# Seven products for eight in the first keys and queries of a linear attention, and output products moved out of crowded rounds

## The chip, the cores and the metric

The kernel runs on one core of a Trainium2 chip. The metric is the device time of one execution in microseconds (us). Engines are named as in the profile: PE is the matrix engine TensorE, PEld its weight loads, DVE is VectorE, ACT is ScalarE, POOL is GpSimd, SP is the engine that issues most transfers. All data are 32-bit floats; the profile counts two matmul instructions for each product that the program asks for.

## The reference

Four layers work one after the other on x of shape (4, 512, 64, 64): four images, 512 channels, 4096 pixels. Cut to what matters:

```python
# layer 0: softmax attention with 64 channels, all pixels against all pixels
t = einsum('oc,bchw->bohw', w_qkv, x)
key_, query, value = ...                       # 64 channels each
attn = softmax(einsum('bdk,bdq->bkq', key_, query), axis=1)
x = scale * (w_out @ (value @ attn)) + x
# layer 1: 1x1, 3x3, 1x1 convolutions (512 -> 128 -> 128 -> 512), whose weights are
# mixed from 8 experts by a router on the mean of x; batch norm, relu, residual
x = relu(bn(conv3(relu(bn(conv2(relu(bn(conv1(x)))))))) + x)
# layer 2: linear attention with 64 channels
Q = softplus(Wq @ x + bq);  K = softplus(Wk @ x + bk);  V = Wv @ x + bv
x = x + gamma * (Q @ (K @ V)) / (Q @ (K.sum(-1) + EPS))
# layer 3: a projection to 2 x 512 channels, two discounted running sums, a gate
x = x + gamma3 * x_gate * sigmoid(cumsum_w(cumsum_h(x_scan)))
```

## The kernel before

The kernel holds one image in SBUF at a time, as four tiles `xs[0..3]` of 128 partitions x 4 channel groups x 1024 pixels (a "pair" of blocks of 512 pixels). Three double banks of PSUM (`pair_psum`) and two single ones (`bank`) go round among all products. PE's order is the program's; that of DVE and ACT is the program's in the stretches named `manual_schedule` and a scheduler's elsewhere. The start:

```python
    for queue, k in ((nc.scalar, 0), (nc.sync, 2)):
        queue.dma_start(wqkv_sb[:, k:k + 2, :], wqkv_t[:, k:k + 2, :])
    prm_sb = const.tile([P, NPRM], F32, tag="prm", name="prm_sb")
    nc.scalar.dma_start(prm_sb, prm)           # 50 columns of parameters
    ...
    xs = [load_pair(0, pr) for pr in range(NPAIR)]
    ...
    nc.scalar.activation(bn_s, bn_v, AF.Sqrt)  # batch norm from the parameters
    nc.vector.reciprocal(bn_v, bn_s)
```

Layer 0's first pair of keys and queries is already made with Strassen's products (in Winograd's form). Its steps for the first image, where a digit is a product, "v" a value product, "t" a sum of x, "seed" the copy of product 1 to where product 2 is added:

```python
first = ("zero v0:0 1:0 v0:1 1:1 seed v0:2 2:0 v0:3 2:1 t5 5 c11 v1:0 v1:1 t6 v1:2 v1:3 cp01 t7 6 e2 "
         "v2:0 v2:1 t4 7 e3 c22 tr01 n5 4 c21 n6 3 c12 n7 v2:2 v2:3 n4")
```

The attention of layer 0 runs in 16 rounds of eight score tiles each; what a round does after its scores:

```python
for g in range(NPAIR * NT // ROUND):
    for i in range(g * ROUND, (g + 1) * ROUND):
        scores(i)                              # two matmuls, Exp on ACT, sum on DVE
    if 1 < g < 2 + 2 * KC:
        pool(...)                              # one mean on ACT
    ended = None
    while done < (g + 1) * ROUND - (RING - ROUND):
        pr = values(done)                      # two matmuls
        done += 1
        if pr is not None:                     # the last key tile of a pair of query blocks
            ended = pr
            if pr < NPAIR - 2:
                late += [(g + 1, lambda pr=pr, m=m: out_step(pr, m)) for m in range(KC)]
    ...
    if ended is not None:
        sums(ended)                            # den on PE; reciprocal, product, two reductions on DVE
    if late and late[0][0] <= g:
        late.pop(0)[1]()                       # out_step: y on PE, x += y on DVE
```

The end of layer 1 and the head of layer 2:

```python
def conv3(pr, h2):
    for m in range(KC):
        y = pair_psum(f"c3_{b}_{pr}_{m}")
        for h in range(2):
            nc.tensor.matmul(y[:, h, :], wc[:, KC + 9 + m, :], h2[:, h, :], start=True, stop=True)
        xm = xs[pr][:, m, :]
        nc.vector.scalar_tensor_tensor(xm, flat(y), bn_s[:, 2 + m:3 + m], xm, ALU.mult, ALU.add)
        nc.scalar.activation(xm, xm, AF.Relu, bias=bn_t[:, 2 + m:3 + m])

def feature_part(w, pair, z, i, k0, n):        # w: 0 queries, 1 keys
    for kc in range(k0, k0 + n):
        for h in range(2):
            nc.tensor.matmul(z[h * D:(h + 1) * D, i, :], wqk_sb[:, kc, w * D:(w + 1) * D],
                             xs[pair[i]][:, kc, h * NB:(h + 1) * NB], start=kc == 0, stop=kc == KC - 1)

def softplus(w, pair, z, in_parts=False):
    ...
    nc.scalar.activation(e, z, AF.Abs, bias=col(BQ2 + w))
    nc.scalar.activation(pos, z, AF.Relu, bias=col(BQ2 + w))
    nc.scalar.activation(e, e, AF.Exp, scale=-1.0)
    nc.vector.tensor_scalar(u, e, 1.0, None, ALU.add)
    # then Ln on ACT; softplus_end: four DVE operations more

    h2[2] = conv2(2)
    conv3(1, h2[1])
    h2[3] = conv2(3)
    weights = load_quarters(b)
    features(1, (0, 1))()()                    # first keys, with their softplus
    conv3(2, h2[2])
    ...
    rest = features(0, (0, 1))                 # first queries
    with tc.manual_schedule(engines={mybir.EngineType.DVE}):
        key_transpose((0, 1))                  # ktr on PE, kt by DVE
        rest = rest()
        move(0, 0)                             # xtr: transposes of x on PE, then a copy xt
        move_by_halves(0, 1)
        conv3(3, h2[3])
        g = bank(f"g_{b}", (P, C))
        keys = features(1, (2, 3))             # last keys
        rest()
        keys = keys()
        products(0, ahead(1))                  # moves (0,2) and (0,3), then g += kt x xt
        keys()
        ...
```

Of the kernel before, what the change touches and what calls it, by code (L numbers as in the profile page):

```python
# [15 lines left out]
P = 128  # L16
# [30 lines left out]
def unshifted(ctx: ExitStack, tc: tile.TileContext, fits, x, wqkv_t, wout_t, router_t,  # L47
# [19 lines left out]
    def four(name):  # L67
        return fourp.tile([P, 2, NB], F32, tag="four", name=name)

    def block(name, shape=(P, NB)):  # L70
        return blkp.tile(list(shape), F32, tag="blk", name=name)
# [14 lines left out]
    def load_pair(b, pr):  # L86
        if b and pr == NPAIR - 1:
            places[NPAIR - 1:] = places[NPAIR], places[NPAIR - 1]
        t = places[pr]
        src = x[b, :, pr * 2 * NB:(pr + 1) * 2 * NB].rearrange("(kc p) n -> p kc n", p=P)  # L90
        if b == 0:
            for kc in range(KC):
                nc.sync.dma_start(t[:, kc, :], src[:, kc, :])
        else:
            nc.sync.dma_start(t, src)
        return t
# [4 lines left out]
    for queue, k in ((nc.scalar, 0), (nc.sync, 2)):  # L101
        queue.dma_start(wqkv_sb[:, k:k + 2, :], wqkv_t[:, k:k + 2, :])
    prm_sb = const.tile([P, NPRM], F32, tag="prm", name="prm_sb")
    nc.scalar.dma_start(prm_sb, prm)
    def col(i, n=1):
        return prm_sb[:, i:i + n]

    xs = [load_pair(0, pr) for pr in range(NPAIR)]

    a11, a12, a21, a22 = (wqkv_sb[:, k:k + 2, w * D:(w + 1) * D] for w in range(2) for k in (0, 2))  # L110
    wout_sb = const.tile([P, C], F32, tag="wout", name="wout_sb")
# [237 lines left out]
    def layer0(b, xs, pro):  # L349
# [106 lines left out]
        with tc.manual_schedule(engines={mybir.EngineType.Activation}):  # L456
            for g in range(NPAIR * NT // ROUND):
                for i in range(g * ROUND, (g + 1) * ROUND):
                    scores(i)
                if 1 < g < 2 + 2 * KC:  # L460
                    pool(NPAIR - 2 + (g - 2) // KC, (g - 2) % KC)
                if g == 1:
                    pro.key_copies()
                ended = None
                while done < (g + 1) * ROUND - (RING - ROUND):
                    if done == NPAIR * NT - 5:
                        inverse_sums(NPAIR - 1)
                    pr = values(done)
                    done += 1
                    if pr is not None:  # L470
# [3 lines that stand above are left out]
                if b == 0 and g == 1:  # L474
                    router = router_of_values()
                if b == 0 and g == 2:
                    router()
                if ended is not None:
                    sums(ended)
                if late and late[0][0] <= g:  # L480
                    late.pop(0)[1]()
        assert not late

# [60 lines left out]
    def layer1(b, xs, wcq, sel, rw, ex4, ex7):  # L544
# [98 lines left out]
                                     AF.Relu, bias=bn_t[:, 1:2], scale=bn_s[:, 1:2])  # L643
            return h2

        def conv3(pr, h2):
            for m in range(KC):
                y = pair_psum(f"c3_{b}_{pr}_{m}")
                for h in range(2):
                    nc.tensor.matmul(y[:, h, :], wc[:, KC + 9 + m, :], h2[:, h, :], start=True, stop=True)  # L650
# [3 lines that stand above are left out]
# [9 lines left out]
    def layer2(b, xs, sums_of_six, mix_last, conv2, conv3, wcq, qs):  # L663
# [14 lines left out]
        def features(w, pair):  # L678
            z = pair_psum(f"z_{b}_{w}_{pair[0]}")
            for i in range(2):  # L680
                feature_part(w, pair, z, i, 0, KC)
            return lambda: softplus(w, pair, z)

        def softplus(w, pair, z, in_parts=False):
            i = 2 * (len(kts) // 2 % 2)
            e, u = sp[:, i], sp[:, i + 1]
            pos, ln = four(f"pos_{b}_{w}_{pair[0]}"), four(f"ln_{b}_{w}_{pair[0]}")
            nc.scalar.activation(e, z, AF.Abs, bias=col(BQ2 + w))
            nc.scalar.activation(pos, z, AF.Relu, bias=col(BQ2 + w))
            nc.scalar.activation(e, e, AF.Exp, scale=-1.0)  # L690
            nc.vector.tensor_scalar(u, e, 1.0, None, ALU.add)
            def logarithm():
                nc.scalar.activation(ln, u, AF.Ln)
                return lambda: softplus_end(w, pair, e, u, pos, ln)
            return logarithm if in_parts else logarithm()
# [37 lines left out]
        def move(pr, j):  # L733
            xtr = pair_psum(f"xtr_{b}_{pr}_{j}")
            for h in range(2):
                n0 = h * NB + j * P
                for kc in range(KC):
                    nc.tensor.transpose(xtr[:, h, kc * P:(kc + 1) * P], xs[pr][:, kc, n0:n0 + P], ident)  # L738
            xt = four(f"xt_{b}_{pr}_{j}")
            (nc.scalar.copy if j % 2 or (pr > 1 and j) else nc.vector.tensor_copy)(xt, xtr)  # L740
            moved.append(xt)

        def products(pr, between=()):
            for j0 in range(0, TPB, 2):
                for step in [lambda j=j: move(pr, j) for j in (2, 3)] if j0 == 0 else between:
                    step()
                for j in range(j0, j0 + 2):
                    t = pr * TPB + j  # L750
                    xt = moved.pop(0)
                    for h in range(2):
                        nc.tensor.matmul(g[h * D:(h + 1) * D, :], kts[pr][:, j, h * D:(h + 1) * D], xt[:, h, :],  # L753
                                         start=t == 0, stop=t == NPAIR * TPB - 1)

        def ahead(pr):
            return [lambda j=j: move(pr, j) for j in range(2)]

        with tc.manual_schedule(engines={mybir.EngineType.DVE}):
            sums_of_six(0)  # L760
            sums_of_six(1)
            sums_of_six(2)
            mix_last()
            h2 = {0: conv2(0)}
            sums_of_six(3)
            h2[1] = conv2(1)
            conv3(0, h2[0])
        h2[2] = conv2(2)
        conv3(1, h2[1])
        h2[3] = conv2(3)  # L770
        weights = load_quarters(b)
        features(1, (0, 1))()()
        conv3(2, h2[2])


        def invert(pair):
# [14 lines left out]
            q = qs[:, pair[0]:pair[1] + 1, :]  # L791
            nc.vector.tensor_tensor(q, q, nrm, ALU.mult)

        rest = features(0, (0, 1))
        with tc.manual_schedule(engines={mybir.EngineType.DVE}):
            key_transpose((0, 1))
            rest = rest()
            move(0, 0)
            move_by_halves(0, 1)
            conv3(3, h2[3])  # L800
            g = bank(f"g_{b}", (P, C))
            keys = features(1, (2, 3))
            rest()
            keys = keys()
            products(0, ahead(1))
            keys()
            products(1, ahead(2))
            kfold = bank(f"kfold_{b}", (P, NPAIR))
            nc.tensor.matmul(kfold, fold, ks, start=True, stop=True)
            ksum = small.tile([P, 1], F32, tag="ksum", name=f"ksum_{b}")  # L810
            nc.vector.tensor_reduce(ksum, kfold, AX.X, ALU.add)
            for h in range(2):
                r = slice(h * D, (h + 1) * D)
                nc.vector.tensor_scalar(kbd[r, 16 * h:16 * (h + 1)], ones[r, 0:16], ksum[r, :], 1e-6, ALU.mult, ALU.add)
            key_transpose((2, 3))
            inv = invert((0, 1))
            products(2, ahead(3))
            divide((0, 1), inv)
            weights[2]()
            products(3)  # L820
            g_sb = block(f"gsb_{b}", (P, C))
            nc.scalar.copy(g_sb, g)
            gt = block(f"gt_{b}", (P, KC, P))

            late = (0, (2, 3), pair_psum(f"z_{b}_0_2"))
            feature_part(*late, 0, 0, 2)

            gk = pair_psum(f"gk_{b}")
            for kc in range(KC):
                nc.tensor.matmul(gk[:, 0, kc * P:(kc + 1) * P], g_sb[:, kc * P:(kc + 1) * P], fold,  # L830
                                 start=True, stop=True)
            nc.scalar.copy(gt, gk[:, 0, :].rearrange("p (kc c) -> p kc c", c=P))
            feature_part(*late, 0, 2, 2)
            kv = small.tile([P, C], F32, tag="kv", name=f"kv_{b}", bufs=1)
            for i in range(2):
                part = slice(i * C // 2, (i + 1) * C // 2)
                kvp = bank(f"kvp_{b}_{i}", (P, C // 2))
                for kc in range(KC):
                    nc.tensor.matmul(kvp, gt[:, kc, :], wv_sb[:, kc, part], start=kc == 0, stop=kc == KC - 1)
                nc.vector.scalar_tensor_tensor(kv[:, part], bv_sb[:, part], ksum, kvp, ALU.mult, ALU.add)  # L840
# [744 lines left out]
```

## Time and profile before

| | before |
|---|---|
| median of 3 runs | 2655.01 us (2654.95 to 2657.95) |
| span of the profiled execution | 2653.7 us |
| granted clock of PE | 0.999 |
| DVE, ACT busy | 76%, 50% of the span |

The page gives each engine's busy time and, apart from it, the chain of work that ended last. An engine's busy share says little of where time can be had; the chain and the waits of the engine that carries it say more. A line of the timeline reads: start, duration, engine, line of the kernel, operation, tile written <- tiles read, shapes, count, and in brackets the idle time before it and what ended it. Costly groups of the page that the change touches:

```profile
L376 PE MATMUL s<-qv,key 64*128 64x512 f32 x2048 | 458.0, 594 | 5.3 <-DVE x L440 3.2
```

Here the columns are the count, the busy time in us, the mean of one in ns, and the idle time of the engine just before these instructions with what ended most of it: 5.3 us in all before the scores.

### The profile page before, as it was taken

Reading aid. Unit: us, or ns where it says so; the run is one execution under the profiler, and the core shown is the slowest. Engines: PE = TensorE matmul, PEld = TensorE weight load, DVE = VectorE, ACT = ScalarE, POOL = GpSimd, SP = SyncE. Lnnn points to the kernel's source line nnn. Section 1 sums busy time; section 2 is a strip of 40 time slices with the busy share of each in tenths; the row PEclk is TensorE's granted clock in tenths of the full one; section 3 lists DMA queues with packets and bytes.
Section 4 is the critical chain, followed back from the end, with each engine's and each line's share of the span. In section 5 each row is a group of like instructions: output and inputs, shape, how many; then the busy total and the mean of one; then the engine's idle time right before and its main releaser. Section 6 shows DMA issues by size and latency. Waiting matters only on the chain.

```text
span 2653.7 us, 25809 instructions
## 1 busy us (share of the span) xinstructions
PE 2636.2 (99%) x10050; PEld 1116.5 (42%) x10050; DVE 2017.9 (76%) x2272; ACT 1316.2 (50%) x1510; POOL 12.1 (0%) x26
## 2 busy tenths in 40 slices
PE   9999999999999999999999999999999999999998
PEld 3333464344333345444433334544443333554443
DVE  7777866888777786688877778668887777856887
ACT  4554353454555436345556553535555555263545
POOL 1000000000000000000000000000000000000000
PEclk9999999999999999999999999999999999999999
DMA  5000210022200021012220002101121000210001
GB/s 193 1 1 1 103 32 1 27 101 80 80 1 1 1 103 32 1 47 80 80 80 1 1 1 103 32 1 63 64 87 72 0 1 8 97 32 1 32 40 57
DMA packets 34739, 115.17 MB, mean 43 GB/s; under 512 B 3120, under 2 KB 12080, under 8 KB 33072
## 3 DMA queue, kind: packets, MB, share of 16 engines
q1 hardware_dynamic: 34320, 113.21, 11.3%
q8 instruction: 81, 1.33, 0.2%
q14 instruction: 50, 0.41, 0.1%
q10 hardware_dynamic: 288, 0.22, 0.0%
HBM read 79.86 MB, written 33.55 MB: 43 GB/s over the span
## 4 chain that ended last, share of the span: by engine, by line
PE 96%; DVE 2%; ACT 1%; issue 0%; DMA 0%; SPq 0%; ACTq 0%
PE av L391 17%; PE sx L934 16%; PE s L376 16%; PE zy L934 12%; PE z L675 4%; PE c L650 4%; PE c L578 4%; PE c L627 3%; PE wv L852 2%; PE y L435 2%; PE kq L312 2%; PE vv L265 2%; PE g L753 2%; PE xtr L738 2%; PE c2e L627 2%; PE kqz L312 1%
## 5 line engine op out<-in xcount | busy, mean ns | idle before, releaser
L376 PE MATMUL s<-qv,key 64*128 64x512 f32 x2048 | 458.0, 594 | 5.3 <-DVE x L440 3.2
L379 ACT ACTIVATE ring<-s 128x1024 f32<-128x1024 f32 x336 | 317.2, 1050 | 260.3 <-PE s L376 260.3
L384 DVE TENSOR_TENSOR acc<-acc,ring 128x1024 f32<-128x1024 f32 x312 | 382.2, 1225 | 63.2 <-ACT ring L379 35.6
L376 PEld LDWEIGHTS s<-qv,key 64*128 64x128 f32 x2048 | 192.1, 186 | 264.0 <-issue 118.1
L391 PE MATMUL av<-ring,qv 128*64 128x512 f32 x1344 | 302.2, 595 | 0.0
L934 PE MATMUL sx<-t,x 128*128 128x512 f32 x512 | 232.4, 593 | 0.0
L384 DVE TENSOR_TENSOR acc<-acc,x 128x1024 f32<-128x1024 f32 x168 | 205.6, 1224 | 34.7 <-ACT x L379 19.4
L379 ACT ACTIVATE x<-s 128x1024 f32<-128x1024 f32 x176 | 166.7, 1053 | 124.4 <-PE s L376 124.4
L391 PEld LDWEIGHTS av<-ring,qv 128*64 128x64 f32 x1344 | 92.6, 137 | 200.1 <-issue 200.1
L939 ACT COPY zy<-sx 128x512 f32<-128x512 f32 x64 | 36.5, 570 | 253.9 <-PE sx L934 253.9
L391 PE MATMUL av<-x,qv 128*64 128x512 f32 x704 | 159.5, 595 | 0.0
L984 DVE TENSOR_TENSOR_SCAN t<-x,t 128x512 f32<-128x512 f32 x128 | 149.2, 1209 | 1.6
L934 PEld LDWEIGHTS sx<-t,x 128*128 128x128 f32 x512 | 96.7, 190 | 124.6 <-issue 120.9
L943 ACT ACTIVATE e<-sx,prm_sb 128x512 f32<-128x512 f32 x128 | 87.8, 686 | 122.4 <-PE sx L934 122.4
L967 DVE TENSOR_TENSOR_SCAN s<-wc,s 128x512 f32<-128x512 f32 x128 | 146.1, 1202 | 0.0
L973 ACT COPY t<-s 128x1024 f32<-128x1024 f32 x64 | 127.5, 1992 | 29.3 <-DVE s L967 28.7
L990 ACT ACTIVATE s<-t 128x1024 f32<-128x1024 f32 x64 | 125.7, 1990 | 11.2 <-DVE t L984 11.1
L934 PE MATMUL zy<-t,wq 128*128 128x512 f32 x256 | 118.5, 602 | 0.0
L934 PE MATMUL zy<-x,wq 128*128 128x512 f32 x256 | 118.0, 600 | 0.0
L934 PE MATMUL sx<-x,wq 128*128 128x512 f32 x256 | 117.1, 595 | 0.0
L934 PE MATMUL sx<-t,wq 128*128 128x512 f32 x256 | 116.6, 595 | 0.0
L934 PE MATMUL zy<-x,x 128*128 128x512 f32 x256 | 116.3, 594 | 0.0
(227 smaller groups left out, 3451.9 us busy)
## 6 DMA issues: line engine op xcount, KB each, us to landing
out_dram<-s SPq DMA_DIRECT2D x62, 512.0 KB, 2.6
x<-in_x_dram SPq DMA_DIRECT2D x12, 2048.0 KB, 8.4
x<-in_x_dram SPq DMA_DIRECT2D x16, 512.0 KB, 9.7
ex<-in_packed_dram SPq DMA_DIRECT2D x4, 2048.0 KB, 7.7
ex<-in_experts_dram SPq DMA_DIRECT2D x4, 2048.0 KB, 7.9
wq<-in_wproj_t_dram SPq DMA_DIRECT2D x32, 256.0 KB, 5.0
ex<-in_packed_dram SPq DMA_DIRECT2D x4, 1536.0 KB, 6.0
ex<-in_experts_dram SPq DMA_DIRECT2D x4, 1536.0 KB, 6.4
```

The costliest lines, as they stand in the source:

```text
L376: nc.tensor.matmul(s[:, h, :], key[r, kt * P:(kt + 1) * P], qry[r, pr * NB:(pr + 1) * NB], start=True, stop=True)
L379: nc.scalar.activation(p, s, AF.Exp)
L384: nc.vector.tensor_tensor(accs[pr], accs[pr], p, ALU.add)
L391: nc.tensor.matmul(avs[pr][h * D:(h + 1) * D, :], vt[:, kt, :], ring[i % RING][:, h, :], start=kt == 0, stop=kt == NT - 1)
L578: nc.tensor.matmul(y[:, h, :], wc[:, kc, :], xs[pr][:, kc, h * NB:(h + 1) * NB], start=kc == 0, stop=kc == KC - 1)
L627: nc.tensor.matmul(y[:, lo - a:hi - a], u, v[:, lo:hi], start=dy == 1, stop=dy == 2)
L650: nc.tensor.matmul(y[:, h, :], wc[:, KC + 9 + m, :], h2[:, h, :], start=True, stop=True)
L934: nc.tensor.matmul(y, w[:, c, self.kind, self.j * P:(self.j + 1) * P], v[:, c, :], start=c == 0 and k in (1, 5), stop=c == 1, skip_group_c ...
L967: nc.vector.tensor_tensor_scan(self.half(i, h), along[:, self.j + 2 * i, :], self.half(i, h), 0.0, ALU.mult, ALU.add)
L973: nc.scalar.copy(self.t[i].rearrange("p (w r) -> p w r", w=W), self.s[i].rearrange("p (r w) -> p w r", w=W))
L984: nc.vector.tensor_tensor_scan(th, down[:, i, :], th, 0.0, ALU.mult, ALU.add)
L990: nc.scalar.activation(self.s[i].rearrange("p (r w) -> p w r", w=W), tw, AF.Sigmoid)
```

## The change

It has three parts.

1. The first pair's keys and queries of layer 2 are a product of a 2 x 2 matrix of weight blocks (queries and keys by two halves of the channels) and a 2 x 2 matrix of x blocks. They are now made with seven products instead of eight. The sums of blocks are made on DVE. The four steps of the third `conv3` stand between these products, the last `conv3` right behind them, and the softplus of both runs beneath the last `conv3` and the last keys' products. The softplus of the queries takes its buffers from the tile of the sums.
2. In layer 0 an output product no longer stands in a round that has the sums of a finished pair (`elif`), which is to even out the rounds.
3. The load of the parameters is issued by SP behind the first pair of x, not by ACT at the start.

The diff, cut to its core:

```diff
-    nc.scalar.dma_start(prm_sb, prm)
-    xs = [load_pair(0, pr) for pr in range(NPAIR)]
+    xs = [load_pair(0, 0)]
+    nc.sync.dma_start(prm_sb, prm)
+    xs += [load_pair(0, pr) for pr in range(1, NPAIR)]
@@ layer 0, the rounds
                 if ended is not None:
                     sums(ended)
-                if late and late[0][0] <= g:
+                elif late and late[0][0] <= g:
                     late.pop(0)[1]()
@@ layer 2
+        def first_features(between):
+            xa, xb = ((x[:, 0:2, :], x[:, 2:4, :]) for x in xs[0:2])
+            t5, t6 = (xsum[:, i:i + 2].rearrange("p c h n -> p c (h n)") for i in (0, 2))
+            w = block(f"zw_{b}", (P, 4, 2, D))
+            ...
+            nc.vector.tensor_tensor(w5, a21, a22, ALU.add)         # and w6, w7, w3
+            ws = {1: a11, 2: a12, 3: w3, 4: a22, 5: w5, 6: w6, 7: w7}
+            ts = {1: xa[0], 2: xa[1], 3: xb[1], 4: t5, 5: t5, 6: t6, 7: t6}
+            zy, y = pair_psum(f"zz_{b}"), bank(f"zs_{b}")
+            def product(k):
+                to = y if k in (1, 6, 7, 4) else zy[:, 0 if k == 2 else 1, :]
+                for c in range(2):
+                    for h in range(2):
+                        nc.tensor.matmul(to[h * D:(h + 1) * D, :], ws[k][:, c, :], ts[k][:, c, h * NB:(h + 1) * NB],
+                                         start=c == 0 and k in (1, 5), stop=c == 1, skip_group_check=k not in (1, 5))
+            ...
+            sub(t5, xb[0], xa[0])             # two DVE operations of 1024 columns each
+            sub(t6, xb[1], t5)
+            yield
+            product(5)
+            product(1)
+            nc.scalar.copy(zy[:, 0, :], y)
+            sub(t5, xa[1], t6)
+            between(0)
+            product(2)
+            product(6)
+            e2 = copy_out(2)
+            between(1)
+            sub(t6, xb[1], xb[0])
+            between(2)
+            product(7)
+            e3 = copy_out(3)
+            between(3)
+            zq = xsum[:, 2]
+            nc.vector.tensor_tensor(zq[:, 1, :], zy[:, 1, :], e3, ALU.add)
+            product(4)
+            nc.vector.tensor_copy(zq[:, 0, :], y)
+            product(3)
+            nc.vector.tensor_tensor(zy[:, 1, :], zy[:, 1, :], e2, ALU.add)
+            yield zy, zq
         h2[2] = conv2(2)
         conv3(1, h2[1])
+        xsum = bigp.tile([P, 4, 2, NB], F32, tag="big", name=f"xsum_{b}")
+        first = first_features(lambda m: conv3(2, h2[2], (m,)))
+        next(first)
         h2[3] = conv2(3)
         weights = load_quarters(b)
-        features(1, (0, 1))()()
-        conv3(2, h2[2])
+        zk, zq = next(first)
+        rest = softplus(0, (0, 1), zq, places=(xsum[:, 0], xsum[:, 1], zq, xsum[:, 3]))
+        keys = softplus(1, (0, 1), zk)
@@
-        rest = features(0, (0, 1))
         with tc.manual_schedule(engines={mybir.EngineType.DVE}):
-            key_transpose((0, 1))
-            rest = rest()
+            conv3(3, h2[3])
             move(0, 0)
             move_by_halves(0, 1)
-            conv3(3, h2[3])
             g = bank(f"g_{b}", (P, C))
-            keys = features(1, (2, 3))
+            last_keys = features(1, (2, 3))
+            keys()
             rest()
-            keys = keys()
-            products(0, ahead(1))
+            key_transpose((0, 1))
+            move(0, 2)
+            keys = last_keys()
+            products(0, ahead(1), (3,))
             keys()
```

More of the change, by code (lines that the diff above doesn't have):

```diff
@@ L644, in conv2, with conv3 @@
             return h2
-        def conv3(pr, h2):
-            for m in range(KC):
+        def conv3(pr, h2, ms=range(KC)):
+            for m in ms:
                 y = pair_psum(f"c3_{b}_{pr}_{m}")
@@ L682, in features, with softplus @@
             return lambda: softplus(w, pair, z)
-        def softplus(w, pair, z, in_parts=False):
+        def softplus(w, pair, z, in_parts=False, places=None):
             i = 2 * (len(kts) // 2 % 2)
-            e, u = sp[:, i], sp[:, i + 1]
-            pos, ln = four(f"pos_{b}_{w}_{pair[0]}"), four(f"ln_{b}_{w}_{pair[0]}")
+            if places:
+                e, u, pos, ln = places
+            else:
+                e, u = sp[:, i], sp[:, i + 1]
+                pos, ln = four(f"pos_{b}_{w}_{pair[0]}"), four(f"ln_{b}_{w}_{pair[0]}")
             nc.scalar.activation(e, z, AF.Abs, bias=col(BQ2 + w))
@@ L741, in move, with products @@
             moved.append(xt)
-        def products(pr, between=()):
+        def products(pr, between=(), more=(2, 3)):
             for j0 in range(0, TPB, 2):
-                for step in [lambda j=j: move(pr, j) for j in (2, 3)] if j0 == 0 else between:
+                for step in [lambda j=j: move(pr, j) for j in more] if j0 == 0 else between:
                     step()
@@ L767, in layer2, with sub, copy_out @@
             conv3(0, h2[0])
+        def first_features(between):
+            xa, xb = ((x[:, 0:2, :], x[:, 2:4, :]) for x in xs[0:2])
+            t5, t6 = (xsum[:, i:i + 2].rearrange("p c h n -> p c (h n)") for i in (0, 2))
+            w = block(f"zw_{b}", (P, 4, 2, D))
+            a21, a22, a11, a12 = (wqk_sb[:, k:k + 2, i * D:(i + 1) * D] for i in range(2) for k in (0, 2))
+            w3, w5, w6, w7 = (w[:, i] for i in range(4))
+            nc.vector.tensor_tensor(w5, a21, a22, ALU.add)
+            nc.vector.tensor_tensor(w6, w5, a11, ALU.subtract)
+            nc.vector.tensor_tensor(w7, a11, a21, ALU.subtract)
+            nc.vector.tensor_tensor(w3, a12, w6, ALU.subtract)
+            ws = {1: a11, 2: a12, 3: w3, 4: a22, 5: w5, 6: w6, 7: w7}
[7 more added lines that the diff above has]
+                                         start=c == 0 and k in (1, 5), stop=c == 1, skip_group_check=k not in (1, 5))
+            def sub(to, u, v):
+                for c in range(2):
+                    nc.vector.tensor_tensor(to[:, c, :], u[:, c, :], v[:, c, :], ALU.subtract)
+            def copy_out(k):
+                e = block(f"z{k}_{b}")
+                nc.scalar.copy(e, y)
+                return e
+            sub(t5, xb[0], xa[0])
[22 more added lines that the diff above has]
+            yield zy, zq
```

## The prediction

> **What bounds the kernel now.** I read the page's busy shares first, then the chain that ended last, then the waits of PE, then its timeline in the stages that the change touches. From the page, the busy times and the chain's shares:
>
> ```profile
> PE 2636.2 (99%) x10050; PEld 1116.5 (42%) x10050; DVE 2017.9 (76%) x2272; ACT 1316.2 (50%) x1510; POOL 12.1 (0%) x26
> ...
> PE 96%; DVE 2%; ACT 1%; issue 0%; DMA 0%; SPq 0%; ACTq 0%
> ```
>
> PE is the bound nearly everywhere: 96% of the chain is matmul after matmul. So the time is the sum of PE's issue steps plus its few waits, and work on DVE or ACT counts only where PE ends up waiting for it. All waits of PE, in total, times, longest:
>
> ```profile
> PE s L376 <- DVE x L440: 3.2, 8, 0.4
> PE s L376 <- ACT ring L379: 2.1, 8, 0.3
> PE kqz L305 <- POOL ident masks.py:199: 1.5, 1, 1.5
> PE xtr L738 <- DVE xt L740: 1.0, 4, 0.2
> PE vv L265 <- DMA x<-in_x_dram: 0.8, 1, 0.8
> ```
>
> Two attention rounds of each image stall (8 = 2 x 4). One of them, PE's timeline and then DVE's:
>
> ```profile
> 175.71 1.13 PE L435 MATMUL y<-o,wout_sb 64*128 64x512 f32 x4
> 176.68 1.88 PE L376 MATMUL s<-qv,key 64*128 64x512 f32 x8
> 178.82 1.13 PE L376 MATMUL s<-qv,key 64*128 64x512 f32 x4 [0.27 <-ACT ring L379]
> 180.35 4.13 PE L376 MATMUL s<-qv,key 64*128 64x512 f32 x18 [0.40 <-DVE x L440]
> ```
>
> ```profile
> 175.83 3.36 DVE L410 RECIPROCAL rec<-den 128x512 f32<-128x512 f32 x1 [2.71 <-PE den L407]
> 179.10 1.18 DVE L440 SCALAR_TENSOR_TENSOR x<-y,prm_sb,x 128x1024 f32<-128x1024 f32 x1
> ```
>
> The output product y is ready at 176.84, but the DVE instruction that empties its PSUM pair stands behind a reciprocal of 3.36 us until 179.10. With one of three pairs held, the scores run short. PE's timeline at the head of layer 2:
>
> ```profile
> 369.32 1.43 PE L627 MATMUL c2e<-wl,wc 128*128 128x256 f32 x6
> 370.68 7.09 PE L675 MATMUL z<-x,wqk_sb 128*64 128x512 f32 x32
> 377.70 7.13 PE L650 MATMUL c<-h,wc 128*128 128x512 f32 x16
> 384.76 7.09 PE L675 MATMUL z<-x,wqk_sb 128*64 128x512 f32 x32
> 391.78 1.09 PE L714 MATMUL ktr<-ident,k 128*128 128x128 f32 x8
> ...
> 401.42 7.09 PE L675 MATMUL z<-x,wqk_sb 128*64 128x512 f32 x32
> 408.44 1.96 PE L738 MATMUL xtr<-ident,x 128*128 128x128 f32 x16
> 410.33 1.94 PE L753 MATMUL g<-xt,kt 128*64 128x512 f32 x8
> 412.20 1.09 PE L738 MATMUL xtr<-ident,x 128*128 128x128 f32 x8
> 413.53 1.09 PE L738 MATMUL xtr<-ident,x 128*128 128x128 f32 x8 [0.24 <-DVE xt L740]
> ```
>
> No wait stands between 370.68 and 412.20: this stage is pure PE work.
>
> **What the Trainium skill says.** (1) "Trainium Kernel Development and Optimization", Performance Expectations: matmul busy time is a poor measure because matmuls are pipelined. The trace agrees: a matmul here lasts 594 ns, but 32 z matmuls take 7.02 us. I therefore use start-to-start times. (2) "TensorEngine Tiling (Array Packing)", Key Properties: a change of tiling mode drains TensorE. The trace shows its price. Inside a block two 64-column matmuls pass in 0.429 us and one of 128 columns in 0.429 us. The z block takes 7.02 us instead of 32 x 0.2145 = 6.86, the conv block after it 7.06 instead of 16 x 0.429 = 6.86. So an excursion to 64 columns and back costs about 0.35 us. (3) "TensorE: Matmul & The Clock Gate", Architectural detail: ScalarE's and VectorE's queues are strict FIFO, as DVE at 179.10 shows. (4) "DMA: Bandwidth & Descriptors", Queues, rings and completion order: SP and ACT each own a row of rings on the same engines, consumed in ring order. Here x's transfers land mostly 1.28 us apart, at 5.73, 7.51, 8.80, 10.08 and 11.36 us; the longer second step is where the parameters (landed at 5.91) share the engines.
>
> **Part 1, the rounds (elif).** An output product no longer falls into a round that has the sums. The stalling rounds are those with both: the sums of pairs 1 and 2 come with a waiting product, the sums of pair 0 don't, and that round shows no wait. In start-to-start time the two stalled steps measure 0.86 and 0.99 us instead of 0.42: 0.43 + 0.57 = 1.0 us a round (more than the idle time shown, because the pipeline also refills). Two rounds x 4 images x 1.0 = 8.0 us. The moved products go to rounds 9, 13 and 14 (and neighbours), which then look like rounds 5 to 7, where product and pooling stand without a wait. So I count the whole **-8.0 us**.
>
> **Part 2, Strassen.** Before, keys and queries of the first pair are 2 blocks of 32 matmuls; after, 7 products x 8 = 56. Saved: 8 x 0.2145 = 1.72 us an image. The products are cut by single convolution steps into 4 blocks (5 and 1; 2 and 6; 7; 4 and 3). With the last keys that makes 5 excursions instead of 3: +2 x 0.35 = 0.70. Net on PE: -1.0 us an image. Laid out from 370.68 with the same steps, the first products of g end, and xtr of block 1 starts, at 411.2 instead of 412.2.
>
> DVE and ACT get more work, which must fit beneath. DVE: 8 differences of 1024 columns (1.22 each, 9.8), 4 weight sums (some 0.2 in a row, 0.8), 3 PSUM operations of 512 columns (0.69, 2.1): 12.7 us an image. In this stage (356 to 412) DVE is busy 31.4 of 56 us, so there is room in sum; the question is each deadline. Placed by hand in the order in which the built program has them, with the durations of before:
> - Term 5 and 6 are ready at 369, products at 370.7.
> - The seed copy on ACT stands behind the last h2 ReLU (ends 375), done 375.6; product 2 wants it at 376.2. Slack 0.6.
> - Term 7 waits until product 6 has read term 6, done 381.7; product 7 at 383.4.
> - The copy e3 on ACT ends 386.6; product 4 at 387.2.
> - The product's PSUM pair is held from before the last conv2 until the softplus of the keys has read it (395.3). So conv3 has two pairs: the third step of the last conv3 wants its pair at 394.3, DVE frees it at 394.1. Tight, but no wait.
> - The key transpose is at 406.6 and the keys are ready at 404. Its PSUM pair is also that of the second x transpose after it (the allocation of images 0 and 1 says so). PE wants that one 0.87 us after the key transpose ends... and the copy kt takes 1.22 plus about 0.3 of hand-over. That is a **new wait, about 0.7 us** an image, refill included.
> - In return the wait of before at 413.53 goes (0.24 idle, 0.40 in steps): its pair is now emptied about 2 us before PE wants it.
>
> Sum: -1.0 + 0.7 - 0.4 = -0.7 an image, **-2.8 us** for four.
>
> **Part 3, the parameters' load.** It goes behind the first pair's four transfers. The same bytes still precede the second pair's first transfer, so that lands at 11.4 as before, and with it the start of term 5. But the parameters now land near 10 us. ACT's square root waits for them and the seed copy stands behind it: 9.55 becomes about 10.6, while product 2 wants its result at 10.18. DVE's ten small ops on the parameters, which ran 6.54 to 7.48 before, now stand between the two halves of term 5: 0.9 us later. The two delays overlap. Start: **+0.9 us**, once.
>
> **Sum:** 2655.0 - 8.0 - 2.8 + 0.9 = **2645.1 us**.
>
> **Rivals.**
> (a) The head of layer 2 becomes bound by DVE and ACT: two PSUM pairs and in-order queues with slacks of 0.2 to 0.6 us. If one deadline slips by a microsecond, everything behind it on DVE slips too. For it: small slacks, 12.7 us more of DVE in a stage of 56 us. Against: none of my deadlines is missed but one. It would cost 1 to 2 us an image: 2649 to 2653.
> (b) The stalls of the rounds move rather than vanish, because DVE's backlog after the sums (reciprocal 3.36, product and two reductions some 1.9) meets the product one round later. Against: round 5 follows the sums of pair 0 in just this way and has no wait. It would give back up to 8 us: 2653.
> (c) The key transpose's wait doesn't appear, since the copy comes in time, and the start isn't delayed, since the parameters land sooner: 2641 to 2642.
>
> **Range and chances.** Part 1 is measured in the trace and sure to about 1 us. Part 2 may lie between -5 and +3, part 3 between 0 and +1.3. 8 in 10: 2641 to 2650. 2% would be 53 us; nothing here is near that: faster 0.01, same 0.985, slower 0.005.
>
> **What would show it.** Right: no wait of the scores for the output product's DVE step or for the ring; PE's 32-matmul z blocks gone from the head of layer 2 save one, 56 matmuls of 64 columns in four blocks; PE's wait for the copy kt, 4 times, near 0.5 us idle; the seed's product and term 5 waiting at 10 to 15 us; the first scores starting 0.9 us later than 46.5. Wrong: waits of PE for the seed or the copies e2 and e3, or for conv3's DVE step, in all four images (rival a), or scores waiting in rounds 9 and 13 (rival b).

## The result, and the profile after

The changed kernel takes 2647.66 us (median of 6 runs, 2646.06 to 2647.90), against 2654.82 (6 runs, 2653.98 to 2657.95) of the kernel before: a ratio of 0.9971, 95% interval 0.9958 to 0.9984. That is 7.2 us less, where 9.9 less was predicted (2645.1, between 2641 and 2650). Against a threshold of 2% the time is the same; as a gain the 7.2 us are clear of the noise.

The page of the changed kernel, busy times and the chain's shares:

```profile
PE 2629.0 (99%) x10018; PEld 1113.4 (42%) x10018; DVE 2066.5 (78%) x2332; ACT 1320.3 (50%) x1522; POOL 12.2 (0%) x26
...
PE 96%; DVE 2%; ACT 1%; DMA 0%; issue 0%; SPq 0%; DVEq 0%; ACTq 0%
```

PE still carries 96% of the chain. It is busy 7.2 us less; DVE has 48.6 us more to do (12.1 an image), and of that only DVE's part in two new waits of PE reaches the time. All waits of PE in the changed kernel, in total, times, longest:

```profile
PE den L408 <- DVE acc L385: 2.5, 4, 0.9
PE xtr L742 <- DVE kt L720: 1.8, 4, 0.4
PE kqz L306 <- POOL ident masks.py:199: 1.5, 1, 1.5
PE kqz L313 <- ACT kqz L318: 1.1, 1, 1.1
PE vv L266 <- DMA x<-in_x_dram: 0.4, 1, 0.4
```

The sixteen waits of the scores are gone. Two of the new lines were expected: the wait for the key transposes' copy kt, and the one for the seed copy. The first was not: den, the sums of the last pair of query blocks, now waits for DVE once in each image. PE's timeline at the head of layer 2 of the first image:

```profile
368.29 1.43 PE L628 MATMUL c2e<-wl,wc 128*128 128x256 f32 x6
369.65 1.94 PE L791 MATMUL zz<-xsum,zw 128*64 128x512 f32 x8
371.42 1.89 PE L791 MATMUL zs<-x,wqk_sb 128*64 128x512 f32 x8
373.24 1.98 PE L651 MATMUL c<-h,wc 128*128 128x512 f32 x4
375.15 1.94 PE L791 MATMUL zz<-x,wqk_sb 128*64 128x512 f32 x8
...
398.54 7.09 PE L676 MATMUL z<-x,wqk_sb 128*64 128x512 f32 x32
405.56 1.09 PE L718 MATMUL ktr<-ident,k 128*128 128x128 f32 x8
406.49 1.04 PE L742 MATMUL xtr<-ident,x 128*128 128x128 f32 x8
407.97 1.09 PE L742 MATMUL xtr<-ident,x 128*128 128x128 f32 x8 [0.44 <-DVE kt L720]
408.99 1.94 PE L757 MATMUL g<-xt,kt 128*64 128x512 f32 x8
410.86 1.97 PE L742 MATMUL xtr<-ident,x 128*128 128x128 f32 x16
```

The products stand without a wait up to 407.97. The price of a change of tiling can be seen in their steps: between the products 5 and 1 (zz to zs at 371.42), where the tile changes but not the tiling, two matmuls still pass in 0.43 us; where products and conv3 meet, the steps beside the change are 0.47 to 0.53 us, some 0.35 us in all for one excursion. The stage from the first product to the first xtr of block 1 takes 41.21 us (369.65 to 410.86); before, it took 41.52 (370.68 to 412.20), and the wait of 0.24 us right behind it is gone too.

Since PE is the chain, the distances between first matmuls on PE show where the time went. From the timelines, in us:

| | first scores | layer 0's attention (first scores to conv1), image 0; 1; 2 | conv1 to layer 2's first value product (wv), image 0 | last matmul to the end of the span |
|---|---|---|---|---|
| before | 46.47 | 252.05; 250.48; 250.48 | 150.04 | 8.89 |
| changed | 47.00 | 250.50; 249.27; 248.91 | 149.27 | 8.07 |

From layer 2's value product to the next image's scores both take 258.75 (before, the first image took 258.94). Image 3 repeats image 2 (250.48 before, 248.91 changed). So the stages that the change touches have moved, and no other stage between them. The end of the span varies from run to run: the kernel with all three repairs (below) has 8.69 us there in one execution and 7.71 in another.

### The profile page after: what moved, and what is told of

Its sections match the earlier page's. It is cut to its first block, busy times and chain, and to the rows that moved or that the text cites. A ratio compares the mean times of both kernels' runs of the same rounds, so it can differ in the third digit from the quotient of the medians.

```text
span 2644.3 us, 25822 instructions
## 1 busy us (share of the span) xinstructions
PE 2629.0 (99%) x10018; PEld 1113.4 (42%) x10018; DVE 2066.5 (78%) x2332; ACT 1320.3 (50%) x1522; POOL 12.2 (0%) x26
## 4 chain that ended last, share of the span: by engine, by line
PE 96%; DVE 2%; ACT 1%; DMA 0%; issue 0%; SPq 0%; DVEq 0%; ACTq 0%
PE sx L997 16%; PE av L392 16%; PE s L377 16%; PE zy L997 12%; PE c L651 4%; PE c L579 4%; PE c L628 3%; PE wv L915 3%; PE y L436 2%; PE g L757 2%; PE z L676 2%; PE kq L313 2%; PE vv L266 2%; PE xtr L742 2%; PE kqz L313 2%; PE c2e L628 2%
```

## The experiments

**Each part alone.** The three parts of the change, each put into the kernel before by itself, and a measurement of the tiling's price, on one chip (the kernel before: 2654.99 us, 48 runs).

The rounds alone:

```diff
-                if late and late[0][0] <= g:
+                elif late and late[0][0] <= g:
```

> The kernel before with the elif alone. Theory: the two stalled rounds of each image go (-8.0 us in start-to-start time), but the last output product now stands two rounds later, the router's small operations on its mean fall into the last round's sums, and PE waits for them before den, 4 times, about 0.8 us each with refill (+3.2): 2654.8 - 4.8 = 2650.0, with that wait of den in the trace. Rival: the wait of den in the changed kernel comes from the Strassen part, and the rounds alone give the whole -8.0: 2646.8, without a wait of den.

Measured: 2649.27 us, ratio 0.9976 (0.9968 to 0.9985): 5.7 us less, where 4.8 was expected. PE's waits:

```profile
PE den L407 <- DVE acc L384: 2.1, 4, 0.5
PE kqz L305 <- POOL ident masks.py:199: 1.5, 1, 1.5
PE xtr L738 <- DVE xt L740: 0.9, 4, 0.2
PE vv L265 <- DMA x<-in_x_dram: 0.5, 1, 0.5
```

The wait of den comes with the rounds and not with Strassen's products, so the rival falls. DVE's timeline at the end of layer 0 of the first image, kernel before:

```profile
261.25 5.21 DVE L384 TENSOR_TENSOR acc<-acc,ring 128x1024 f32<-128x1024 f32 x4
270.02 5.21 DVE L384 TENSOR_TENSOR acc<-acc,ring 128x1024 f32<-128x1024 f32 x4 [3.55 <-ACT ring L379]
275.33 5.21 DVE L384 TENSOR_TENSOR acc<-acc,x 128x1024 f32<-128x1024 f32 x4
```

and with the rounds evened out:

```profile
265.98 1.28 DVE L440 SCALAR_TENSOR_TENSOR x<-y,prm_sb,x 128x1024 f32<-128x1024 f32 x1 [2.20 <-PE y L435]
267.19 0.08 DVE L440 DVE_READ_ACCUMULATOR x<-y,prm_sb,x 128x1 f32 x1
267.31 0.17 DVE L486 TENSOR_REDUCE pooled<-pool 128x4 f32<-128x16 f32 x1
...
268.77 0.23 DVE L493 SCALAR_TENSOR_TENSOR base<-wr_sb,osum,base 128x8 f32<-128x8 f32 x1
268.92 5.21 DVE L384 TENSOR_TENSOR acc<-acc,ring 128x1024 f32<-128x1024 f32 x4
274.23 5.21 DVE L384 TENSOR_TENSOR acc<-acc,x 128x1024 f32<-128x1024 f32 x4
```

Before, DVE waits 3.55 us for the last round's exponentials and sums them as they come. Now the last output product (round 14) is added at 265.98, and with its mean the router's seven small operations become ready and run at once, down to 268.92. The eight sums start late, stay late since they follow each other without a gap, and den waits for the eighth. It is the router's operations that make them late, and not the product's own addition: ACT's first exponential of the round is ready near 267.9 (four in 3.77 us from 266.84, 1.05 us each), by when the addition is over (267.27). ACT's and PE's timeline:

```profile
266.84 3.77 ACT L379 ACTIVATE ring<-s 128x1024 f32<-128x1024 f32 x4 [7.56 <-PE s L376]
...
279.50 1.08 PE L407 MATMUL den<-acc,ones 128*64 128x512 f32 x4 [0.54 <-DVE acc L384]
```

By PE's steps in image 1, the scores got 2.31 us shorter and the wait of den cost 0.71.

Strassen's products and the new order of layer 2 alone (the changed kernel without the `elif`, and with the parameters' load at the start):

> The kernel before with the Strassen products and the new order of layer 2 alone. Theory: -0.76 us an image (1.72 saved, 0.70 for two more excursions to 64 columns, +0.6 for the wait for kt, -0.4 for the wait that goes): 2654.8 - 3.0 = 2651.8; the stalls of the scores stay (8 and 8), the wait for kt is there 4 times, no wait of den. Rival: the part alone hurts elsewhere (a later stage, or the wait of den comes with it): 2654 to 2655, with that wait shown.

Measured: 2651.80 us, ratio 0.9987 (0.9981 to 0.9994): 3.2 us less, where 3.0 was expected. PE's longest waits:

```profile
PE s L376 <- DVE x L440: 3.2, 8, 0.4
PE s L376 <- ACT ring L379: 2.1, 8, 0.3
PE xtr L741 <- DVE kt L719: 1.8, 4, 0.4
```

The stalls of the scores stay, the wait for kt is there and den doesn't wait, so the rival falls. The stretch from conv1 to layer 2's value product takes 149.28 instead of 150.04 us: 0.76 an image.

The parameters' load alone:

```diff
-    nc.scalar.dma_start(prm_sb, prm)
-    xs = [load_pair(0, pr) for pr in range(NPAIR)]
+    xs = [load_pair(0, 0)]
+    nc.sync.dma_start(prm_sb, prm)
+    xs += [load_pair(0, pr) for pr in range(1, NPAIR)]
```

> The kernel before with the parameters' load behind the first pair of x alone. Theory: the seed copy waits behind the square root, PE waits 1.1 us for it, and the first scores start at 47.0 instead of 46.5 us: +0.5, 2655.3. Rival: the earlier first transfer (x lands 0.4 us sooner) makes up for it and the time is the same within 0.2 us, or a later wait absorbs it.

Measured: 2656.03 us, ratio 1.0002 (0.9993 to 1.0010), which doesn't settle the sign. The trace shows the mechanism. DVE, ACT and PE in its timeline:

```profile
9.79 0.29 DVE L156 TENSOR_SCALAR bn_v<-prm_sb 128x1 f32<-128x1 f32 x3 [3.08 <-DMA prm_sb<-in_prm_dram]
10.12 0.21 ACT L157 ACTIVATE bn_s<-bn_v 128x6 f32<-128x6 f32 x1 [7.65 <-DVE bn_v L156]
10.23 0.58 ACT L318 COPY kqz<-kq 128x512 f32<-128x512 f32 x1
...
10.86 1.08 PE L313 MATMUL kqz<-x,wqkv_sb 128*64 128x512 f32 x4 [0.71 <-ACT kqz L318]
```

The parameters land near 9.8 us, the square root runs at 10.12, the seed copy right behind it, and PE has waited 0.71 us. The first scores stand at 46.89; what the start loses is taken up in the last section, as the start varies by itself.

The last keys' products cut into three blocks, nothing else:

```diff
-            conv3(3, h2[3])
-            keys = features(1, (2, 3))
+            z = pair_psum(f"z_{b}_1_2")
+            conv3(3, h2[3], (0,))
+            feature_part(1, (2, 3), z, 0, 0, 2)
+            conv3(3, h2[3], (1,))
+            feature_part(1, (2, 3), z, 0, 2, 2)
+            conv3(3, h2[3], (2, 3))
+            feature_part(1, (2, 3), z, 1, 0, KC)
+            keys = lambda: softplus(1, (2, 3), z)
```

> The kernel before, with the last keys' products cut into three blocks of 8, 8 and 16 matmuls between the last conv3's steps: the same matmuls, two more excursions to 64 columns an image. Theory: a change of tiling costs PE about 0.35 us an excursion, +0.70 an image, +2.8: 2657.6, without a new wait of PE. Rival: the price hides beneath other waits or weight loads when the blocks are small: within 0.5 us of 2654.8.

Measured: 2658.37 us, ratio 1.0013 (1.0005 to 1.0021): 3.4 us more, with the kernel before's list of waits unchanged. PE's timeline:

```profile
394.64 1.88 PE L650 MATMUL c<-h,wc 128*128 128x512 f32 x4
396.45 1.94 PE L675 MATMUL z<-x,wqk_sb 128*64 128x512 f32 x8
398.32 1.98 PE L650 MATMUL c<-h,wc 128*128 128x512 f32 x4
400.24 1.94 PE L675 MATMUL z<-x,wqk_sb 128*64 128x512 f32 x8
```

Eight z matmuls from 396.45 to 398.32 take 1.87 us, of which 8 x 0.2145 = 1.72 are work. The stretch from conv1 to layer 2's value product takes 150.80 instead of 150.04 us: 0.38 for each excursion, with no wait in sight. Here a change of tiling is issue time on PE that no list of waits shows.

By their medians the three parts alone add up to -5.7 - 3.2 + 1.0 = -7.9 us; the whole change took 7.2 us on the first chip and 8.3 on another. So they don't hinder each other by more than the noise.

**Repairs of the changed kernel.** Each takes away one of its three waits (on another chip than the parts; the kernel before: 2655.16 us). The expectations start from 2647.7 us; on this chip the changed kernel took 2646.95 us later (below), so that is what the repairs are compared with.

```diff
                 elif late and late[0][0] <= g:
-                    late.pop(0)[1]()
+                    for _ in range(2 if g == 10 else 1):
+                        late.pop(0)[1]()
```

> The changed kernel, but round 10 of the attention takes two output products, so that the last of them stands in round 13 and not 14. Theory: the router's operations on the mean then run a round earlier, DVE is done with the last sums in time, and the wait of den (4 times, 0.8 us each in steps) goes: 2647.7 - 3.2 = 2644.5; two products in one round cost no wait of the scores, as neither stands behind a reciprocal. Rival: DVE's backlog comes from the sums themselves, the wait stays, or two products in a round starve the scores as before: 2647 to 2652.

Measured: 2644.52 us, ratio 0.9960 (0.9947 to 0.9974): 2.4 us below the changed kernel, where 3.2 was expected. The number 2644.5 was hit because its starting point was too high. The wait of den is gone, and DVE has its gap before the last sums again:

```profile
254.94 0.17 DVE L488 TENSOR_REDUCE pooled<-pool 128x4 f32<-128x16 f32 x1
...
261.86 5.21 DVE L385 TENSOR_TENSOR acc<-acc,ring 128x1024 f32<-128x1024 f32 x4
269.56 5.21 DVE L385 TENSOR_TENSOR acc<-acc,ring 128x1024 f32<-128x1024 f32 x4 [2.49 <-ACT ring L380]
```

The router's operations run at 254.94, a round earlier. Layer 0's attention takes 248.47 us in image 2 instead of 248.91: 0.44 less, not 0.7, because behind the two products one step of the scores takes 0.62 us instead of 0.43 and the next one 0.53; over the four images the attention is 2.1 us shorter. So the cause of den's wait is where the last product stands, with the router's operations behind it, and not DVE's load from the sums.

```diff
-            ktr = pair_psum(f"ktr_{b}_{pair[0]}")
+            ktr = [bank(f"ktr_{b}_{pr}") for pr in pair]   # for the first pair of pairs; two copies kt
@@
             key_transpose((0, 1))
+            g = bank(f"g_{b}", (P, C))                     # taken after them, not before
```

> The changed kernel, but the first key transposes go to the two single banks, copied out half by half, so that the x transpose after them doesn't need their pair. Theory: PE's wait for kt (4 times 0.6 us in steps) goes: 2647.7 - 2.4 = 2645.3. Rival: g needs one of the single banks and waits for the same copy, so the wait only moves to g: 2647.7.

Measured: 2643.51 us, ratio 0.9956 (0.9942 to 0.9970): 3.4 us below the changed kernel. PE's timeline:

```profile
405.29 1.09 PE L719 MATMUL ktr<-ident,k 128*128 128x128 f32 x8
406.22 1.91 PE L747 MATMUL xtr<-ident,x 128*128 128x128 f32 x16
408.06 1.94 PE L762 MATMUL g<-xt,kt 128*64 128x512 f32 x8
```

All transposes run on and g doesn't wait either. From conv1 to layer 2's value product: 148.61 instead of 149.28 us. The rival is out. By this stretch the repair is worth 4 x 0.67 = 2.7 us. In this trace the first image's later layers take 0.73 us longer (259.48 instead of 258.75); in the later kernels with the same repair they don't.

The third repair puts the parameters' load back on ACT at the start, as in the kernel before.

> The changed kernel with the parameters' load back on ACT at the start. Theory: the wait for the seed copy goes and the first scores start 0.5 us earlier: 2647.2. Rival: no difference.

Measured: 2645.59 us, ratio 0.9966 (0.9952 to 0.9979). The wait for the seed is gone and the first scores stand at 46.42. The time is 1.4 us below the changed kernel on the same chip, whose first scores stand at 47.14. So the start is worth 0.7 us in these traces; another 0.3 lies in image 1's attention, where den waits 0.5 instead of 0.9 us, and the rest stays open.

> The changed kernel with all three: two output products in round 10, the first key transposes in single banks, the parameters' load at the start. Theory: the sums add up, -3.2 - 2.4 - 0.5: 2641.6. Rival: a wait behind them takes over and half of it is lost: 2644.5.

Measured: 2641.43 us, ratio 0.9948 (0.9934 to 0.9962): 5.5 us below the changed kernel. That the number was hit is partly luck: by the stages the parts are 2.1, 2.7 and 0.7 us, not 3.2, 2.4 and 0.5, and the starting point was 0.7 us too high. No wait of PE is left behind the start:

```profile
PE kqz L305 <- POOL ident masks.py:199: 1.5, 1, 1.5
PE vv L265 <- DMA x<-in_x_dram: 0.6, 1, 0.6
```

**Side by side.** The changed kernel, the three repairs together, and these with the two products of round 10 set apart, on the chip of the repairs (the kernel before: 2655.23 us):

> The changed kernel itself, on the same chip as the next two, for a comparison that no change of chip blurs: 2647, with the waits for den, kt and the seed as in its first trace.

> The kernel with all three repairs once more, beside the changed one: by PE's time between the same points, 4 x (0.45 + 0.67) = 4.5 us less than the changed kernel, and about 0.5 at the start: 2642. Rival: chip and day made half of the earlier distance, 2644.

> All three repairs, but of the two output products of round 10 one stands behind the scores and the other behind the values. Theory: the two steps of the scores that are 0.19 us long after two products in a row (once an image) go: -0.8, 2641. Rival: behind the scores no PSUM pair is free, as ACT is still at the exponentials, and PE waits there instead: the same or up to 1 us more.

```diff
                     scores(i)
+                if g == 10:
+                    late.pop(0)[1]()
```

Measured: 2646.95 us (ratio 0.9969, 0.9956 to 0.9981), 2641.69 (0.9949, 0.9935 to 0.9963) and 2639.20 (0.9944, 0.9930 to 0.9958). The repairs are worth 5.3 us. Setting the products apart takes 0.30 us an image from layer 0's attention (248.56 to 248.26 in image 1), where 0.2 was expected, so 1.2 of the 2.5 us are explained by it. The rest is not shown: the two kernels' runs overlap (2641.13 to 2642.79 against 2638.46 to 2642.54), and their traces differ otherwise only at the start and the end, which vary by themselves. PE's timeline of round 10 in the last kernel:

```profile
190.46 7.08 PE L376 MATMUL s<-qv,key 64*128 64x512 f32 x32
197.37 1.02 PE L435 MATMUL y<-o,wout_sb 64*128 64x512 f32 x4
198.33 1.94 PE L391 MATMUL av<-x,qv 128*64 128x512 f32 x8
```

The product stands right behind the scores without a wait, so the rival of a missing PSUM pair falls. This kernel beats both: 16.0 us below the kernel before, 7.8 below the changed one.

## Why the prediction was right, and where not

- **Part 1, the rounds, -8.0.** The mechanism was right: the product behind the reciprocal held a PSUM pair, and without it the scores run on. Their gain was even undersized: 2.31 us an image instead of 2.0, as the step behind each stalled one takes 0.53 us instead of 0.43, too, which the prediction left out. The step that failed is "which then look like rounds 5 to 7 ... So I count the whole -8.0 us". Round 14 doesn't look like them, as the last product of layer 0 releases the router's operations in front of the last sums. That gave 0.71 us back (1.06 in image 1 of the changed kernel, in both of its traces; why it is more there stays open). Together the rounds alone bring 1.54 to 1.57 us an image, -6.2, and -5.9 in the changed kernel. The prediction was sure of this part to about 1 us; it missed by 2.
- **Part 2, Strassen, -2.8.** 0.76 an image, -3.0. The terms hold: excursions 0.38 instead of 0.35; the wait for kt is 0.44 idle, 0.61 in steps, instead of 0.7; the old wait, 0.40, is gone. No other deadline was missed: layer 2's seed and e3 copies, term 7 and conv3's two pairs all came in time (PE's list has no wait for them), and rival (a) didn't happen.
- **Part 3, the load, +0.9.** The size was off: the first scores are 0.53 us later. The wait for the seed is there (1.07 us, 1.24 in steps). But the first matmul on x starts 0.46 us sooner (5.40 instead of 5.86), which the prediction left out, and term 5, whose delay of 0.9 us was counted with the seed's, holds PE nowhere now; before, PE's step at 13.24, behind the first half of term 5, took 0.69 us instead of 0.43. One reading of the prediction falls here, too. It laid the long step between x's first two landings (5.73 to 7.51, 1.78 us) to the parameters' load; with that load behind the pair's four transfers the step is as long (5.26 to 7.09), and with it in front it can be 1.29 us (5.72 to 7.01, with all three repairs). What makes it long stays open.
- **The sum.** In the changed kernel's trace, -5.9 - 3.0 + 0.5 = -8.4 by PE's stages; the medians say -7.2, and -8.3 on the second chip. The difference is within what start and end vary from run to run (1.8 and 1.0 us between two traces of one kernel).
- **Rival (b)**, that the stalls move with DVE's backlog, did not happen as it was written: the scores wait nowhere, neither in round 9 nor in 13, and it is not the work behind a reciprocal that got in the way. It was right only in that a wait for DVE comes in place of the stalls: den's, at the end of the layer, which takes a third of the gain.

## What to carry to other kernels

When one engine is the whole chain, add up its issue steps and its waits, and check the work given to others only at its deadlines. Before moving an operation to a later slot, look up what becomes ready with it: here it was not the product but the chain of small operations on its result that got in front of the last sums. A saving in matmuls that comes in more and smaller pieces must pay for each change of the array's tiling; here that took 0.76 of the 1.72 us saved an image.

## What the runs showed that was not expected

- The start of one and the same program varies, and in the pair of traces with the largest distance most of that is PE's clock. The kernel with all three repairs has its first scores at 46.94 us in one profiled execution and at 48.78 in another, while each image's stages agree within 0.02 us. PE's timeline in the second:

```profile
6.13 1.97 PE L265 MATMUL vv<-x,wqkv_sb 128*64 128x512 f32 x4 [0.89 <-DMA x<-in_x_dram]
7.87 1.95 PE L312 MATMUL kq<-x,wqkv_sb 128*64 128x512 f32 x4
...
11.11 1.04 PE L312 MATMUL kq<-x,wqkv_sb 128*64 128x512 f32 x4
11.97 1.04 PE L265 MATMUL vv<-x,wqkv_sb 128*64 128x512 f32 x4
```

The block at 6.13 takes 1.74 us from its start to the next one's, the same block of four at 11.11 takes 0.86. The trace's record of the granted clock begins, at full clock, at 10.93 us, where the long steps end; in the first execution it begins at 7.50, and only one block is long there (5.86 to 7.55). In the other profiled executions it begins between 4.65 and 7.25 us. So starts should be compared between traces in which it begins at about the same time. Four such pairs, with the parameters' load behind the first pair of x and at the start, have their first scores at 47.00 and 46.47, 46.89 and 46.17, 46.72 and 46.06, 47.14 and 46.42: the load costs 0.5 to 0.7 us. In a fifth pair it is 1.4, where x's second transfer landed 2.8 us behind its first.
- A stall of the scores costs more than its idle time: 0.67 us idle a stalled round (0.27 + 0.40), but 1.16 us in steps (2.31 for the two rounds of an image). A stalled step is the idle time and one whole matmul (0.27 + 0.59 = 0.86, and 0.40 + 0.59 = 0.99), where matmuls without a wait start 0.43 us apart; and the step behind each is 0.53 us long.
